# A transformer block on one core: pair sums of the last attention unit split between GpSimd and VectorE, and the projection's operands prepared in pieces

## The chip, the core and the metric

The kernel runs on one NeuronCore of a Trainium2 chip. TensorE (PE) does the matrix products, VectorE (DVE), ScalarE (ACT) and GpSimd (POOL) the elementwise work, and SyncE (SP) and ScalarE issue most of the DMA transfers. The metric is the device time of one launch in microseconds. Time before: 2572.67 us, the median of 3 runs (2571.6 to 2576.87). The profile is of one further execution of its own.

## The reference

The input x has B = 2 elements of T = 2048 rows and D = 512 columns, in float32; there are H = 16 heads of 32 columns.

```
mod = silu(condition) @ Wada + bada
sh_a, sc_a, gt_a, sh_m, sc_m, gt_m = split(mod, 6)
xm = layernorm(x) * (1 + sc_a) + sh_a
q, k, v = heads(xm @ Wqkv)
attn = softmax(where(causal, q @ k.T * 32**-0.5, -inf))
x = x + gt_a * ((attn @ v) @ Wproj + bproj)
xm = layernorm(x) * (1 + sc_m) + sh_m
x = x + gt_m * (gelu(xm @ W1 + b1) @ W2 + b2)
```

## The kernel before

**Stages.** For each batch element: queries, keys and values (class `Qkv`), attention (`attention_phase`, L481), and the output projection with the residual sum (`project_phase`, L849). The projection of element 0 runs together with the beginning of element 1's queries and keys, that of element 1 with the beginning of the feed-forward part, which comes last for both elements.

**Attention units.** The 16 heads form four groups c of four heads, and the 2048 query rows four blocks i of 512. A unit is one pair (c, i), in the order of `units` (L258); the last four are (3, 0), (3, 2), (3, 1), (3, 3), so `last_order` is 0, 2, 1, 3. The document counts blocks in this order: block 1 is i = 0, block 2 is i = 2, block 3 is i = 1, block 4 is i = 3. A unit goes through its key tiles of 128 rows in steps. The last unit has 15 steps, 0 to 14: twelve full ones, the diagonal one (12), a pair (13) and a half (14).

**A step** (`scores_t`, L488): for each head, PE first writes minus the row maximum into a PSUM bank of the tag st (from `fold`, which L466 makes once for each unit), then adds the transposed scores; ScalarE takes the exponential into a tile e (L526; 12 buffers, so three steps), and on the diagonal GpSimd masks it (L531). Two steps later PE multiplies e with the values into o. For the row sums, GpSimd adds the tiles of two neighbouring steps (`pair_sums`, L548, the addition is L551; 6 buffers ee), and PE sums the result over the rows into sm. `finish` (L561) copies o and sm out and stores them (od and sd in DRAM).

**Row maxima.** The scores in the other orientation are made ahead of their unit, piece by piece between the products of earlier steps (`score`, `bank`): PE writes a tile s, and VectorE takes its maximum (L407, on the diagonal L402). The last unit has none of this work left.

**What the projection needs.** The result of each block is divided by its row sums before it is multiplied with Wproj. `inverses` (L316) loads a block's sums as a tile r, inverts them (L328), stores them to DRAM (L329) and loads them back broadcast over the 32 columns of each head, in four transfers of 256 KB (L331), into a tile rb or into an old query tile (`old_queries`; the tag qst has 4 buffers). `prefetch` (L341), called at step 3 of the last unit, loads Wproj, the bias, x rows and the results of blocks 1 and 2, calls `inverses` for both on SyncE's queue, and multiplies each block as a whole (L373). `gate_weights` (L375), called at step 7, multiplies the bias and the four pieces of Wproj with the gate row (L378, L380; PE makes that row by a small product). In `project_phase` the inverses of blocks 3 and 4 are made on ScalarE's queue (L873) and multiplied in pieces of 512 columns (L892); for each 128 rows GpSimd adds the bias to x (L880), PE makes four products into ps_o, VectorE adds both (L887) and takes the statistics of the next normalization, and SyncE stores the result (L889).

**What sets the order.** A scheduler places the instructions of each engine by when it expects their operands; every instruction that passes through `mm`, `transpose` or `act` keeps the program's order on its engine. Each engine works through its queue in that order. DMA transfers of both queues take eight completion semaphores in turn: each waits for the one eight places before it.

Of the kernel before, what the change touches and what calls it, by code (L numbers as in the profile page):

```python
# [8 lines left out]
F32 = mybir.dt.float32  # L9
# [18 lines left out]
def dit_block_kernel(  # L28
# [32 lines left out]


    nc = tc.nc
    B, T, D = x.shape
# [10 lines left out]
    E_BUFS = 12  # L75
    EE_BUFS = 6
    AHEAD = 2
# [194 lines left out]
    class Row:  # L272
# [31 lines left out]
        def load_queries(self, u):  # L304
# [9 lines left out]
            self.qst[u] = t  # L314

        def inverses(self, i, rb, queue):  # L316

            sums, inv = [
                d[self.b][i].rearrange("c h (p q) -> (c h p) q", p=P // (C * HC))
                for d in (sd, rd)
            ]
            r = bp.tile([P, C * HC * QB // P], F32, tag="r", name="r", bufs=2)
            queue.dma_start(r, sums)
            nc.vector.reciprocal(r, r)  # L328
            queue.dma_start(inv, r)  # L329
            for c in range(C):  # L330
                queue.dma_start(  # L331
                    rb[:, c, :],
                    rd[self.b][i][c].unsqueeze(1).to_broadcast([HC, HD, QB]),
                )
# [6 lines left out]
        def prefetch(self):  # L341
# [27 lines left out]
            nc.sync.dma_start(self.at_s[1], od[b][last_order[1]])  # L369
            for k in range(2):  # L370
                rb = self.old_queries()
                self.inverses(last_order[k], rb, nc.sync)
                nc.vector.tensor_tensor(self.at_s[k], self.at_s[k], rb, ALU.mult)  # L373

        def gate_weights(self):  # L375

            ps = rows_of(ps_sp, 0, self.b, "s")
            nc.vector.tensor_tensor(bgate, bgate, ps, ALU.mult)  # L378
            for c in range(C):
                nc.vector.tensor_tensor(  # L380
                    self.wproj[:, c, :], self.wproj[:, c, :], ps, ALU.mult
                )

# [97 lines left out]
    def attention_phase(row):  # L481
        b, vv, kst, qst = row.b, row.vv, row.kst, row.qst
        with pool(f"att{b}") as ap, pool(
# [4 lines left out]
            def scores_t(u, step, n):  # L488
# [26 lines left out]
                for h in range(HC):  # L515
# [11 lines left out]
                    if tiles[0][0] >= i * TQ:  # L527

                        d = e.rearrange("p (t k) -> p t k", k=P)[:, 0 : TQ : TQ - 1, :]
                        d = d[:, : len(tiles), :]  # L530
                        nc.gpsimd.affine_select(  # L531
                            d, d, pattern=[[0, len(tiles)], [1, P]],
                            compare_op=ALU.is_ge, fill=0.0,
                            base=0, channel_multiplier=-1,
                        )
# [11 lines left out]

            def pair_sums(es0, es1):  # L548
                out = new_sums()
                for h in range(HC):  # L550
                    nc.gpsimd.tensor_tensor(out[h], es0[h], es1[h], ALU.add)  # L551
                return out
# [50 lines left out]
            for u, (c, i) in enumerate(units):  # L603
# [5 lines left out]
                for n_step, tiles in enumerate(steps_of[u]):  # L609
# [10 lines left out]
                    if u + 1 < len(units) and row.rows_made == u + 1:  # L620
                        if last:
                            row.score(row.count(cum[-1], u + 1))
                        make_rows = last or (ready > u + 1 and n_step >= 1)
                    if u == len(units) - 1 and n_step == 3:
                        row.prefetch()
                    if u == len(units) - 1 and n_step == 7:
                        row.gate_weights()
                    flush(now)
# [33 lines left out]
                    else:  # L662
                        ee = pair_sums(even, es)
                        pending.append(
# [184 lines left out]
    def project_phase(row, psum, between):  # L849
# [5 lines left out]
        with pool(f"proj{b}") as pp:  # L855
# [3 lines left out]
            for k, i in enumerate(last_order):  # L859
# [6 lines left out]
                for t in range(TQ):  # L866
                    if n in (0, TQ - 1):
                        d = 2 + n // (TQ - 1)
                        rbs[d] = (
                            row.old_queries() if d == 2  # L870
                            else pp.tile([P, C, QB], F32, tag="rb", name="rb")
                        )
                        row.inverses(last_order[d], rbs[d], nc.scalar)  # L873
                    nt = b * NT + i * TQ + t
# [502 lines left out]
```

## Time and profile before

| | us |
|---|---|
| median of 3 runs | 2572.67 |
| profiled execution: its own time | 2566.7 |
| profiled execution: span from the first to the last instruction | 2564.6 |
| PE busy in the span | 2502.6 (98%) |
| VectorE busy | 1301.8 (51%) |
| ScalarE busy | 895.4 (35%) |
| GpSimd busy | 845.1 (33%) |

The mean clock granted to PE is 0.989 of full speed. Times in the profile count from the start of the span; lines such as L551 are lines of the kernel before. The last two units of element 0 lie at about 690 to 826 us and its projection at 826 to 890; those of element 1 at 1550 to 1687 and 1687 to 1757. A busy PE is not PE at its peak, since matmuls are pipelined; what an edit is worth is read from the places where PE is idle or its clock is low, and from what ended the wait there.

### The profile page before, as it was taken

The page shows a single profiled execution, that of the slowest core. Times are in us where ns is not written, and L with a number is a line of the kernel's source. Part 1 is how long each engine was busy: PE and PEld are TensorE (multiplying, and loading weights), DVE is VectorE, ACT ScalarE, POOL GpSimd, SP SyncE. Part 2 cuts the span into 40 slices and gives each one's busy share as a digit, 9 for nine tenths or more (in the row PEclk, how much of TensorE's full clock was granted, in tenths as well). Part 3 has the DMA queues.
Part 4 walks back from the last instruction along what each step waited for, and adds up shares of the span by engine and source line. Part 5 has one row for each costly group of instructions (what it writes and reads, how often), then busy time and mean ns, then how long its engine had stood idle before and what let it go on. Part 6 is the DMA issues. An engine that isn't in the chain of part 4 may idle for free.

```text
span 2564.6 us, 31548 instructions
## 1 busy us (share of the span) xinstructions
PE 2502.6 (98%) x11361; PEld 1185.5 (46%) x11361; DVE 1301.8 (51%) x2732; ACT 895.4 (35%) x1667; POOL 845.1 (33%) x1038
## 2 busy tenths in 40 slices
PE   7999999999999999999999999899999999999998
PEld 3445445445443444454454445344444444444443
DVE  3455657666551635556665756245353344334424
ACT  1213455455545011254545454513312312311310
POOL 0001454544556366245545554632101100100100
PEclk9999999999999999999999999999999999999999
DMA  6645123041211798640414112144233332322422
GB/s 219 207 125 146 38 56 77 22 108 42 92 49 50 238 294 284 203 95 22 108 42 102 34 40 81 64 160 143 76 99 106 107 107 90 129 89 76 138 82 94
DMA packets 131718, 277.87 MB, mean 108 GB/s; under 512 B 13109, under 2 KB 41821, under 8 KB 127466
## 3 DMA queue, kind: packets, MB, share of 16 engines
q1 hardware_dynamic: 122818, 248.29, 32.7%
q0 software_dynamic: 5376, 23.07, 2.6%
q10 hardware_dynamic: 3368, 4.50, 0.5%
q8 instruction: 89, 1.46, 0.2%
q14 instruction: 67, 0.55, 0.1%
HBM read 201.90 MB, written 73.92 MB: 108 GB/s over the span
## 4 chain that ended last, share of the span: by engine, by line
PE 91%; DMA 4%; DVE 2%; issue 1%; POOL 1%; ACT 1%; SPq 0%; ACTq 0%; DVEq 0%; POOLq 0%
PE st L190 20%; PE ps_y L190 15%; PE ps_h L190 15%; PE o L190 10%; PE s L190 9%; PE ps_qk L190 8%; PE sm L190 6%; PE ps_v L190 4%; PE ps_o L190 2%; DMA rb<-r 1%; PE ps_xt L198 1%; DMA qst<-r 1%; DVE mx L407 1%; POOL ee L551 1%; PE ps_o L198 0%
## 5 line engine op out<-in xcount | busy, mean ns | idle before, releaser
L526 ACT ACTIVATE e<-st 128x512 f32<-128x512 f32 (+1 forms) x1152 | 575.5, 576 | 556.7 <-PE st L190 511.1
L551 POOL TENSOR_TENSOR ee<-e 128x512 f32<-128x512 f32 x384 | 489.3, 1305 | 423.1 <-ACT e L526 271.5
L407 DVE TENSOR_REDUCE mx<-s 128x1 f32<-128x512 f32 x616 | 413.8, 687 | 285.4 <-PE s L190 284.2
L190 PE MATMUL s<-kst,qst 128*128 128x512 f32 (+3 forms) x1058 | 451.3, 446 | 15.7 <-DVE mx L407 12.9
L190 PE MATMUL st<-qst,kst 128*128 128x512 f32 (+3 forms) x1280 | 435.4, 389 | 0.0
L190 PE MATMUL o<-e,vv 128*32 128x512 f32 (+3 forms) x2560 | 295.2, 542 | 0.0
L402 DVE CUSTOM_DVE_ANT_0 junk<-s,causal 128x384 bf16<-128x384 f32 (+3 forms) x442 | 211.3, 478 | 148.8 <-PE s L190 139.5
L190 PE MATMUL ps_h<-sx,w 128*128 128x512 f32 x640 | 286.7, 592 | 0.0
L190 PE MATMUL ps_y<-sh,w 128*128 128x512 f32 x640 | 277.8, 594 | 0.0
L190 PEld LDWEIGHTS st<-qst,kst 128*128 128x128 f32 x1280 | 227.8, 190 | 87.2 <-issue 62.8
L190 PEld LDWEIGHTS s<-kst,qst 128*128 128x128 f32 x1058 | 198.8, 189 | 140.5 <-DVE mx L407 57.5
L531 POOL TENSOR_SCALAR_AFFINE_SELECT e<-e 128x128 f32<-128x128 f32 (+1 forms) x384 | 124.9, 333 | 395.6 <-ACT e L526 389.2
L1148 POOL TENSOR_TENSOR c<-c 128x512 f32<-128x512 f32 x32 | 40.8, 1274 | 615.7 <-DVE c L1110 606.3
L190 PE MATMUL ps_qk<-xmT,wqkv 128*128 128x512 f32 x512 | 240.6, 598 | 2.2 <-DVE xmT L246 2.2
L1110 DVE TENSOR_TENSOR h<-c,ps_h 128x512 f32<-128x512 f32 x128 | 88.1, 688 | 231.4 <-PE ps_h L190 231.4
L190 PEld LDWEIGHTS ps_h<-sx,w 128*128 128x128 f32 x640 | 121.1, 190 | 150.2 <-issue 149.7
L190 PEld LDWEIGHTS ps_y<-sh,w 128*128 128x128 f32 x640 | 121.3, 191 | 148.5 <-issue 147.1
L190 PE MATMUL st<-fold,sel 32*128 32x512 f32 (+1 forms) x1152 | 162.4, 484 | 6.2 <-ACT e L526 3.8
L1134 ACT ACTIVATE h<-h,cols 128x512 f32<-128x512 f32 x128 | 92.4, 722 | 181.6 <-DVE h L1110 181.6
L190 PEld LDWEIGHTS st<-fold,sel 32*128 32x128 f32 x1152 | 64.6, 183 | 191.7 <-ACT e L526 110.0
L190 PEld LDWEIGHTS ps_qk<-xmT,wqkv 128*128 128x128 f32 x512 | 94.7, 191 | 97.6 <-issue 90.3
L190 PE MATMUL ps_v<-wqkv,xmT 128*128 128x512 f32 x256 | 122.8, 595 | 2.1 <-ACT xmT L251 2.1
(122 smaller groups left out, 2261.6 us busy)
## 6 DMA issues: line engine op xcount, KB each, us to landing
qst<-q SPq DMA_DIRECT2D x128, 256.0 KB
w<-w1d SPq DMA_DIRECT2D x34, 896.0 KB
w<-w2d SPq DMA_DIRECT2D x28, 1024.0 KB
kst<-k SPq DMA_DIRECT2D x24, 1024.0 KB
q<-hl SPq DMA_DIRECT2D x32, 512.0 KB
k<-hl SPq DMA_DIRECT2D x32, 512.0 KB
kst<-k SPq DMA_DIRECT2D x32, 256.0 KB
o<-ot SPq DMA_DIRECT2D x32, 256.0 KB
```

The costliest lines, as they stand in the source:

```text
L190: return tc.keep_in_program_order(nc.tensor.matmul(*args, **kw))
L198: return tc.keep_in_program_order(nc.tensor.transpose(dst, src, ident[:n, :n]))
L402: nc.vector.tensor_tensor_reduce(junk[:, :w], s[:, :w], causal[:, QB - w :], 1.0, MASKED, ALU.add, ALU.max, m,)
L407: nc.vector.tensor_reduce(m, s[:, :w], axis=AX.X, op=ALU.max)
L526: act(nc.scalar.activation(e[:, :w], sts[h][:, :w], AF.Exp))
L531: nc.gpsimd.affine_select(d, d, pattern=[[0, len(tiles)], [1, P]], compare_op=ALU.is_ge, fill=0.0, base=0, channel_multiplier=-1,)
L551: nc.gpsimd.tensor_tensor(out[h], es0[h], es1[h], ALU.add)
L1110: nc.vector.tensor_tensor(dst, x, y, op)
L1134: nc.scalar.activation(d, d, AF.Gelu, bias=col(r_b1 + chunk, 1))
L1148: nc.gpsimd.tensor_tensor(c1_, c1_, c2_, ALU.subtract)
```

## The change

In the last unit of each element VectorE does the pair sums of heads 1 and 3, and GpSimd those of heads 0 and 2. `prefetch` only loads, the sums of block 3 among them. A new function `prepare` spreads the rest over the steps of the last unit: at step 5 the reciprocals of blocks 1 to 3 with their stores, and the gate row; at steps 5 to 8 one piece of Wproj each; at step 7 the broadcasts for blocks 1 and 2; at steps 9 to 12 one piece of each of the two blocks. `inverses` is split into `load_sums`, `invert` and the broadcasts; for block 4 all three stay in the projection. The reciprocals, the multiplies, the masks and the pair sums keep the program's order on their engines. The tag ee has 12 buffers instead of 6, and r has 3 instead of 2.

```diff
@@ -73,7 +74,7 @@
     NG = T // MT
     LAG = 2
     E_BUFS = 12
-    EE_BUFS = 6
+    EE_BUFS = 12
     AHEAD = 2
     const = ctx.enter_context(tc.tile_pool(name="const", bufs=1))
@@ -313,20 +314,22 @@
                 )
             self.qst[u] = t
+        def load_sums(self, i, queue):
+            r = bp.tile([P, C * HC * QB // P], F32, tag="r", name="r", bufs=3)
+            queue.dma_start(
+                r, sd[self.b][i].rearrange("c h (p q) -> (c h p) q", p=P // (C * HC))
+            )
+            return r
+        def invert(self, i, r, queue):
+            act(nc.vector.reciprocal(r, r))
+            queue.dma_start(
+                rd[self.b][i].rearrange("c h (p q) -> (c h p) q", p=P // (C * HC)), r
+            )
         def inverses(self, i, rb, queue):
-            sums, inv = [
-                d[self.b][i].rearrange("c h (p q) -> (c h p) q", p=P // (C * HC))
-                for d in (sd, rd)
-            ]
-            r = bp.tile([P, C * HC * QB // P], F32, tag="r", name="r", bufs=2)
-            queue.dma_start(r, sums)
-            nc.vector.reciprocal(r, r)
-            queue.dma_start(inv, r)
             for c in range(C):
                 queue.dma_start(
                     rb[:, c, :],
@@ -367,19 +370,28 @@
                 else:
                     nc.sync.dma_start(self.next_s[t], x1d[t])
             nc.sync.dma_start(self.at_s[1], od[b][last_order[1]])
-            for k in range(2):
-                rb = self.old_queries()
-                self.inverses(last_order[k], rb, nc.sync)
-                nc.vector.tensor_tensor(self.at_s[k], self.at_s[k], rb, ALU.mult)
-        def gate_weights(self):
-            ps = rows_of(ps_sp, 0, self.b, "s")
-            nc.vector.tensor_tensor(bgate, bgate, ps, ALU.mult)
-            for c in range(C):
-                nc.vector.tensor_tensor(
-                    self.wproj[:, c, :], self.wproj[:, c, :], ps, ALU.mult
-                )
+            self.r_s = [self.load_sums(i, nc.sync) for i in last_order[:3]]
+        def prepare(self, n):
+            if n == 3:
+                self.prefetch()
+            elif n == 5:
+                for k in range(3):
+                    self.invert(last_order[k], self.r_s[k], nc.sync)
+                self.ps_gate = rows_of(ps_sp, 0, self.b, "s")
+                act(nc.vector.tensor_tensor(bgate, bgate, self.ps_gate, ALU.mult))
+            elif n == 7:
+                self.rb_s = [self.old_queries() for _ in range(2)]
+                for k in range(2):
+                    self.inverses(last_order[k], self.rb_s[k], nc.sync)
+            if 5 <= n < 5 + C:
+                w = self.wproj[:, n - 5, :]
+                act(nc.vector.tensor_tensor(w, w, self.ps_gate, ALU.mult))
+            elif 9 <= n < 9 + C:
+                for k in range(2):
+                    d, r = self.at_s[k][:, n - 9, :], self.rb_s[k][:, n - 9, :]
+                    act(nc.vector.tensor_tensor(d, d, r, ALU.mult))
         def width(self, u, h, t, kb):
             last = kb == units[u][1]
@@ -528,10 +540,12 @@
                         d = e.rearrange("p (t k) -> p t k", k=P)[:, 0 : TQ : TQ - 1, :]
                         d = d[:, : len(tiles), :]
-                        nc.gpsimd.affine_select(
-                            d, d, pattern=[[0, len(tiles)], [1, P]],
-                            compare_op=ALU.is_ge, fill=0.0,
-                            base=0, channel_multiplier=-1,
+                        act(
+                            nc.gpsimd.affine_select(
+                                d, d, pattern=[[0, len(tiles)], [1, P]],
+                                compare_op=ALU.is_ge, fill=0.0,
+                                base=0, channel_multiplier=-1,
+                            )
                         )
                     es.append(e)
                     if h >= HC - n:
@@ -545,10 +559,12 @@
                     for _ in range(HC)
                 ]
-            def pair_sums(es0, es1):
+            def pair_sums(u, es0, es1):
                 out = new_sums()
                 for h in range(HC):
-                    nc.gpsimd.tensor_tensor(out[h], es0[h], es1[h], ALU.add)
+                    vector = u == len(units) - 1 and h % 2
+                    engine = nc.vector if vector else nc.gpsimd
+                    act(engine.tensor_tensor(out[h], es0[h], es1[h], ALU.add))
                 return out
             def products(dst, lhs, es, q0, at, first, last):
@@ -621,10 +637,8 @@
                         if last:
                             row.score(row.count(cum[-1], u + 1))
                         make_rows = last or (ready > u + 1 and n_step >= 1)
-                    if u == len(units) - 1 and n_step == 3:
-                        row.prefetch()
-                    if u == len(units) - 1 and n_step == 7:
-                        row.gate_weights()
+                    if u == len(units) - 1:
+                        row.prepare(n_step)
                     flush(now)
                     if make_rows:
                         row.rows(u + 1)
@@ -660,7 +674,7 @@
                     elif n_step % 2 == 0:
                         even = es
                     else:
-                        ee = pair_sums(even, es)
+                        ee = pair_sums(u, even, es)
                         pending.append(
                             (
                                 now + LAG + 1,
@@ -870,6 +884,12 @@
                             row.old_queries() if d == 2
                             else pp.tile([P, C, QB], F32, tag="rb", name="rb")
                         )
+                        if d == 3:
+                            row.invert(
+                                last_order[d],
+                                row.load_sums(last_order[d], nc.scalar),
+                                nc.scalar,
+                            )
                         row.inverses(last_order[d], rbs[d], nc.scalar)
                     nt = b * NT + i * TQ + t
                     if k == 0:
```

## The prediction

> **What bounds the kernel now.** I read the page first (TensorE, PE, is busy 98% of a 2564.6 us span), then PE's busy time and granted clock in slices of 5 us over the whole span, then the chain of waits and the timelines of the slices where PE is not full. Outside the start and the end of the program, PE is idle for more than 0.6 us at a time in three places per batch element that the change touches, and after each the granted clock is below 1 for a while. Columns: slice, length, PE, PEld, DVE, ACT, POOL busy, clock, DMA share, GB/s.
>
> ```profile
> 740.00:745.00 5.00, 2.64 (x23) 1.48 (x15) 0.00 (x0) 2.06 (x4) 2.94 (x3) 1.00 0.25 97
> 745.00:750.00 5.00, 1.42 (x6) 0.67 (x10) 4.30 (x6) 0.00 (x0) 4.05 (x2) 0.56 0.00 2
> 750.00:755.00 5.00, 5.00 (x33) 2.47 (x37) 2.44 (x7) 3.09 (x6) 0.00 (x0) 0.76 0.16 56
> ...
> 800.00:805.00 5.00, 3.54 (x23) 1.38 (x19) 0.00 (x0) 1.93 (x4) 5.00 (x5) 1.00 0.02 9
> 805.00:810.00 5.00, 4.59 (x21) 1.46 (x21) 0.00 (x0) 2.42 (x5) 3.23 (x3) 0.70 0.02 3
> ...
> 855.00:860.00 5.00, 3.96 (x13) 1.76 (x11) 1.61 (x3) 0.00 (x0) 0.29 (x1) 1.00 0.49 178
> 860.00:865.00 5.00, 2.70 (x6) 1.56 (x7) 3.31 (x7) 0.00 (x0) 4.54 (x4) 0.67 0.64 202
> 865.00:870.00 5.00, 5.00 (x9) 2.03 (x8) 4.91 (x12) 0.00 (x0) 0.59 (x1) 0.65 0.86 302
> ```
>
> To be seen: stall A (742 to 749, in the last unit but one), stall B (803 to 806, inside the last unit), stall C (859 to 863, in the projection). Batch element 1 has the same three at 1601 to 1609, 1663 to 1666 and 1716 to 1722. The chain of waits says what ended A and B (start, us, what):
>
> ```profile
> 734.35 10.98 DMA qst<-r
> ...
> 745.62 0.13 DVE kst L373
> 745.75 2.10 issue
> 747.85 0.69 DVE mx L407
> 748.54 0.04 issue
> 748.58 1.39 PE s L190 x2
> ...
> 797.31 1.94 POOL kst L880 x2
> ...
> 802.28 2.46 POOL ee L551 x2
> 804.74 0.02 issue
> 804.76 0.61 ACT e L526
> ```
>
> A: VectorE's queue holds the multiply L373 in the middle of the score maxima (L407). It waits for the broadcast inverses, and PE waits for the maxima behind it. B: GpSimd was given the four bias adds (L880) between its pair sums (L551); the sums come late, their e buffers stay taken, and the exponentials and PE wait. C has two causes. In element 0, PE waits for L887, that for L880, that for an x load which SyncE issued at 854.12, when the third broadcast of block 4's inverses (rb) had landed. In element 1, VectorE stands in L892 until 1716.55 for the fourth rb, with L887 behind it.
>
> **The Trainium skill.** "TensorE: Matmul & The Clock Gate", What's actually happening: an idle window of some 3.4 us puts PE on half clock, and a busy one releases it. The trace agrees in kind: 0.56 and 0.76 behind stall A. "DMA: Bandwidth & Descriptors", Why a DMA increments its semaphore by 16 and not by 1: a transfer uses as many engines as divide its slowest dimension, the lowest-numbered ones. An inverse broadcast has 4 heads as slowest dimension, so all of them share 4 of 16 engines: the slice 740 to 745 shows a share of 0.25 and 97 GB/s. "SBUF — State Buffer", Who interferes with whom: a VectorE instruction with two SBUF inputs excludes a GpSimd one that reads SBUF. The trace agrees: four sums take 5.0 us alone and 6.98 us (from 742.07) beside the 2.31 us multiply.
>
> **The change, part by part.** What each stall costs: idle plus (1 - clock) x busy of the slow slices.
> - A: element 0: 2.36 + 3.58 = 5.94 idle, 0.44 x 1.42 + 0.24 x 5 = 1.82 of clock; element 1: 5.93 + 1.64. Sum 15.3 us.
> - B: 1.87 + 1.63 and 1.88 + 1.50. Sum 6.9 us.
> - C: element 0 3.34 + 2.64 = 6.0; element 1 4.88 + 2.12 = 7.0.
>
> Together 35.2 us: the ceiling.
>
> *Multiply and inverse out of the score work.* L373 (two of 2.3 us) becomes eight multiplies of 512 columns at steps 9 to 12 of the last unit, after the last maximum. In the compiled order of the changed kernel nothing on VectorE before the last unit's fold waits for a DMA of this preparation. A goes wholly: **-15.3**. Next late there would be VectorE itself, but it is busy 3.2 to 4.4 us of 5 in this stage, so it keeps up. Bounds: -13 (the clock part only half real) to -15.3.
>
> *Half of the sums to VectorE.* 24 sums a unit; GpSimd keeps 12. A pair of steps takes 6.3 to 6.6 us (exponentials from 777.75 to 784.03). GpSimd's load per pair falls from 4 x 1.25 = 5.0 to 2.5, plus 2 x about 0.65 for the exclusion, 3.8; the four bias adds (1.25 each) now stand two before and two after one sum. VectorE's sum is priced as L892 (512 columns, two SBUF inputs, 0.68): 1.4 per pair. The sum of step 5 must be read before step 7's exponential needs the buffer. Counted from the unit's first exponential (771.18), steps start about 0, 3.4, 6.6, 9.7, 12.9, 16.3, 19.4, 22.8, 26.0, 29.4, 32.5, 35.9, 39.0, 42.5, 45.4. The gate product of the bias (bgate) is ready at about 18.5, two adds end at 21.3, the sum behind them at 22.6; head 2 of step 7 needs it at 23.8. It fits by 1.2 us. I leave 0.4 for both elements: **-6.5**, bounds -3 and -6.9.
>
> *VectorE's queue in the last unit.* Behind the three reciprocals stand bgate, the weights and all later sums. The third needs block 3's sums: stored at 6.5, and loaded by about 10.2 (1.9 us from store to load and at most 1.85 to the reciprocal in this trace); VectorE reaches it at 12.4 to 13.9. No wait. SyncE then issues three stores and eight broadcasts; the first goes at about 14.4 (1.44 us after a store of inverses). Four broadcasts took 12.7 us from the first issue (732.61) to the last landing (745.33), of which 10.5 at 97 to 100 GB/s: 2.65 each. All eight use the same engines: landings at about 19, 22, 25, 27.5 and 30, 33, 35.5, 38. The multiplies ask for block 2's first piece before the sum of step 9 (29.4 to 31.5), and for its last at 38. Just in time: **0**, bounds 0 and +4.
>
> *Block 3's broadcasts.* They leave ScalarE's queue behind step 12's exponentials (about 41.1), since their buffer is the one that the multiplies have read; three issues of 0.53 stand before step 13's exponentials, and the last before step 14's. ScalarE is idle 1.1 to 1.5 us a step, and in the trace these issues ran beside exponentials: **0**, bounds 0 and +2. They land by 4 us into the projection; their use is at 8.
>
> *Block 4's inverses in program order.* The reciprocal moves from behind one or two to behind three blocks of 128 rows: from 5.2 (831.69 - 826.48) to about 14 in element 0, from 6.7 to about 12 in element 1. With it move the store and four broadcasts. Element 0: stage by stage the inverse store lands near 17, rb 0 to 2 at about 24, 27, 30. But the x loads now wait for rb 0, 1 (or for none) instead of rb 2, 3 (each DMA waits for the one eight before it, and the order moved): x at 28 instead of 33. L887 can go at about 31; PE needed it at 32.5. Stall nearly gone: **-5.0**, bounds -6 and +2. Element 1: the broadcasts start at 14, not 8.7. Before, they took 20.7 us, at 4.1 each under other loads: (256 KB + a sixteenth of 3.4 MB) per engine at 25 GB/s is 19 us. With some 2.5 MB beside them now, 16.6 + 2.1: the last lands at about 33, not 29.4. Four multiplies (L892) that wait for it stand before the second L887 of the second block, and PE's transpose needs the normalization some 3.4 us behind: PE goes on at 36.4 instead of 34.3. Stall C of element 1 grows: **+2.8** with its clock, bounds -7 and +6.
>
> *Buffers, and the fixed order of GpSimd.* Twelve sum buffers remove GpSimd's waits for PE (1.5 to 1.8 us before a group of sums), which ended nothing on PE. Masks now come after four pending sums instead of two: 2.5 us later, with two steps of 3.4 to 3.8 us in hand. **0**, bounds 0 and +2.
>
> Sum: -15.3 - 6.5 - 5.0 + 2.8 = **-24.0 us**. Against the profiled execution: 2566.7 - 24.0 = 2542.7. The median of the runs shown, 2572.67, is 6.0 above that execution; so **2549 us**.
>
> **The rivals.**
> R1, both C stalls vanish: the rb broadcasts of element 1 run at 2.65, land at 27, and the x loads no longer wait for them. For it: 8 x 2.65 is what the trace shows when nothing else loads. Against: loads of 2 MB fall into the same time. -15.3 - 6.9 - 6 - 7 = -35: 2538.
> R2, B stays in another form: a VectorE sum behind a waiting reciprocal or multiply holds the e buffers as L880 did, or GpSimd loses more to the exclusion. For it: margins of 1.2 us. -15.3 + 0 - 3 + 3 = about -15: 2557.
> R3, slower: block 3's first broadcast sits in ScalarE's in-order queue, waiting for VectorE's last multiply of block 1 and for block 2's broadcasts; the last two steps' exponentials are behind it, and PE behind them. It costs as soon as the eighth broadcast lands after 41. At 4.9 us a broadcast instead of 2.65 it lands at 14.4 + 2.1 + 39 = 56, PE stands 15 us in each element: -24 + 30 = +6, 2579. For it: 4.1 each was seen in the projection. Against: in the last unit the DMA share is 0.02 to 0.26, so nothing slows them.
> R4, no change: a wait of the same size as A appears in the projection, about 2572.
>
> **How the numbers follow.** Forecast 0.58, R1 0.14, R2 0.18, R3 0.06, R4 0.04. The forecast, R1 and R2 are faster by over 0.2% (5 us, about what a measurement of this kernel can tell from no change): 0.90; same 0.04; slower 0.06. The range takes in R1 and R2: 2537 to 2561.
>
> **What would show it.** A right: no slice under 4.9 of PE in the last unit but one, and VectorE's only waits there are for PE. B right: no exponential waits for a sum in the last unit. Broadcast step right: eight landings 2.65 us apart, share 0.26 for 21 us. C: in element 0 PE full around 33 us into the projection, in element 1 a stall of 5 to 9 us ended by L892 waiting for rb. Wrong if ScalarE waits at its broadcasts, or if sums on VectorE stand behind a DMA.

## The result, and the profile after

The changed kernel takes 2557.38 us, the median of 5 runs (2556.07 to 2561.76), beside 2571.74 us for the kernel before (5 runs, 2570.12 to 2576.87): 0.9943 of its time, with a 95% interval of 0.9929 to 0.9958. That is 14.4 us faster; 24.0 were forecast. The profiled execution took 2558.56 us, with a span of 2556.7 us. The profiled execution of the kernel before was faster than all its timed runs (2566.7 against 2570.12 and more), so the two profiles differ by 7.9 us only, and the sum of the steps has to be compared with 7.9, not with 14.4. In which stage the timed runs of the kernel before lose the other 5 us, no trace shows.

PE's time can be cut at its own events into stages that add up to the span: the 15 attention units ahead of the last one of each element (from the first turned maximum of the first unit to that of the last), the last unit (to the first ps_o), the projection (first to last ps_o). What lies between hardly changes: the start 223.8 and 224.8, queries and keys of element 1 195.5 and 197.0, everything after its projection 811.7 in both. How far one profile can be trusted is seen from the two kernels that were profiled twice (the changed kernel and e9, e7 and e10): they differ by at most 0.9 us in the 15 units, 0.2 in the last unit, 2.4 in the projection and 3.8 in the queries and keys of element 1, which take 195.3 to 203.2 us in the fourteen profiles. The table has all kernels of this study, element 0 / element 1, in us:

| kernel | 15 units | last unit | projection | ratio to before, 95% |
|---|---|---|---|---|
| before | 539.3 / 538.4 | 63.4 / 63.6 | 63.1 / 65.8 | 1 |
| changed | 535.8 / 534.8 | 59.6 / 59.6 | 62.6 / 70.8 | 0.9943 (0.9929 to 0.9958) |
| e1 free reciprocal | 535.2 / 535.0 | 59.6 / 59.6 | 63.1 / 65.3 | 0.9943 (0.9922 to 0.9963) |
| e2 broadcasts by head | 534.5 / 534.4 | 62.2 / 62.2 | 57.9 / 58.7 | 0.9905 (0.9890 to 0.9920) |
| e3 before, 12 buffers | 543.6 / 542.2 | 60.1 / 60.0 | 63.4 / 66.3 | 0.9985 (0.9976 to 0.9994) |
| e4 buffers split | 531.5 / 531.8 | 65.3 / 65.2 | 62.5 / 71.9 | 0.9968 (0.9955 to 0.9980) |
| e5 sums on GpSimd | 534.5 / 535.4 | 71.0 / 71.3 | 63.4 / 70.3 | 1.0044 (1.0030 to 1.0058) |
| e6 before, by head | 533.1 / 534.1 | 66.4 / 66.7 | 57.0 / 58.6 | 0.9942 (0.9928 to 0.9955) |
| e7 buffers by head | 531.7 / 531.8 | 59.7 / 59.6 | 63.9 / 70.4 | 0.9936 (0.9921 to 0.9951) |
| e8 e7 and e2 together | 531.6 / 529.0 | 60.1 / 60.2 | 57.5 / 58.6 | 0.9861 (0.9845 to 0.9878) |
| e9 changed again | 535.0 / 534.9 | 59.8 / 59.6 | 62.5 / 73.2 | 0.9945 (0.9932 to 0.9959) |
| e10 e7 again | 532.3 / 532.7 | 59.6 / 59.6 | 62.4 / 70.2 | 0.9936 (0.9924 to 0.9949) |
| e11 e8 without the moves | 532.9 / 534.8 | 65.9 / 65.7 | 57.5 / 58.7 | 0.9922 (0.9910 to 0.9935) |
| e12 e11, gate at step 5 | 533.7 / 534.3 | 59.4 / 59.5 | 56.8 / 58.6 | 0.9878 (0.9858 to 0.9897) |

The slices of the changed kernel that answer to those of before (slice, length, busy time of PE, PEld, DVE, ACT and POOL, clock, DMA share, GB/s):

```profile
740.00:745.00 5.00, 5.00 (x45) 2.47 (x41) 3.10 (x6) 2.08 (x4) 0.00 (x0) 1.00 0.00 0
745.00:750.00 5.00, 4.98 (x50) 2.52 (x41) 2.69 (x6) 2.76 (x6) 2.75 (x3) 1.00 0.01 3
...
800.00:805.00 5.00, 5.00 (x34) 2.23 (x31) 5.00 (x6) 2.65 (x6) 2.17 (x2) 1.00 0.27 105
...
850.00:855.00 5.00, 2.64 (x10) 1.16 (x8) 1.41 (x2) 0.00 (x0) 1.03 (x1) 1.00 0.56 184
855.00:860.00 5.00, 2.98 (x7) 1.59 (x8) 4.45 (x9) 0.00 (x0) 4.35 (x4) 0.72 0.57 186
```

A and B are gone: PE is full in 740 to 750 and in 800 to 805, at full clock. The unit that held A, the last of the 15, took 59.3 and 59.0 us and takes 51.6 in both elements (from its first turned maximum to that of the next). C is still there, 4.4 us of idle PE in element 0. In element 1 it is 10 us, where it was 4.9:

```profile
1700.00:1705.00 5.00, 3.45 (x9) 1.29 (x7) 0.79 (x2) 0.00 (x0) 0.00 (x0) 1.00 0.82 261
1705.00:1710.00 5.00, 0.00 (x0) 0.00 (x0) 0.59 (x1) 0.00 (x0) 0.00 (x0) 0.71 0.22 85
1710.00:1715.00 5.00, 1.51 (x7) 1.51 (x8) 4.84 (x10) 1.13 (x2) 0.35 (x1) 0.50 0.36 114
```

Its chain of waits (start, us, what; `r<-r` is the store of the inverted sums, `rb<-r` a broadcast of them) reads:

```profile
1687.27 3.61 DMA r<-r
...
1692.75 17.36 DMA rb<-r
...
1710.74 0.68 DVE xt L907
```

The store of the inverses takes 3.6 us, then the last broadcast lands 17.4 us after it was issued, and the normalization of the next rows (L907 of the changed kernel, L887 before) stands on VectorE behind the multiplies that wait for it.

The table shows one thing more, which no step of the forecast had. The unit that held A lost 7.7 and 7.4 us, but the 15 units together lost only 3.5 and 3.6. Two units in each element became longer: both took 52.8 us and take 54.3 (the first of element 0 from 403.15 to 457.48; the expectations below count the second together with the unit of 21.1 us ahead of it, as 74.0 and 75.5). In the first of them PE is idle for 1.07 us, where it was for 0.02. The chain of the changed kernel there:

```profile
451.61 0.22 DVE m L431
451.83 0.20 DVE junk L414
452.03 0.01 DVE mx L414
452.04 0.94 DVE mhl L433
452.98 0.02 issue
453.00 1.21 DVE mhl L434
454.20 0.33 DVE junk L414
```

L433 and L434 split the maxima of the next unit into a rounded part and the rest, 128 x 16 elements each (L421 and L422 before). Their median is 0.17 and 0.18 us, and here they take 0.94 and 1.21. Score maxima stand behind them, and PE behind these. GpSimd's timeline tells what differs. First the changed kernel, then the kernel before:

```profile
449.16 5.01 POOL L567 TENSOR_TENSOR ee<-e 128x512 f32<-128x512 f32 x4 [2.76 <-ACT e L538]
454.11 1.05 POOL L544 TENSOR_SCALAR_AFFINE_SELECT e<-e 128x128 f32<-128x128 f32 x4
```

```profile
447.03 2.53 POOL L551 TENSOR_TENSOR ee<-e 128x512 f32<-128x512 f32 x2 [2.74 <-ACT e L526]
451.14 0.29 POOL L531 TENSOR_SCALAR_AFFINE_SELECT e<-e 128x128 f32<-128x128 f32 x1 [1.58 <-ACT e L526]
...
453.11 2.52 POOL L551 TENSOR_TENSOR ee<-e 128x512 f32<-128x512 f32 x2 [0.19 <-PE sm L190]
```

With 6 buffers the last two sums of the pair of steps wait for PE (sm), and masks go first. The split fell into that gap, at 449.8. With 12 buffers four sums of 1.25 us go in one go, and the split falls among them: L433 is over at 452.98 and L434 at 454.2, when the third and the fourth of the sums end.

The collision itself isn't new. In the kernel before the split is as slow in three other units of each element, in element 0 at 356.5, 507.8 and 659.2 us:

```profile
356.52 1.29 DVE L421 CAST mhl<-m 128x16 fp32r<-128x16 f32 x1
357.85 1.22 DVE L422 TENSOR_TENSOR mhl<-m,mhl 128x16 fp32r<-128x16 f32 x1
```

There no maximum follows it directly on VectorE. The units around it take 59.4 to 59.7 us, and as long in the changed kernel, where the split has no sum beside it. So the collision costs time by its place: the change moved it in front of maxima that PE waits for.

### The profile page after: what moved, and what is told of

The parts are those of the page before. It is cut to its first block, busy times and chain, and to the rows that moved or that the text cites. A ratio compares the mean times of both kernels' runs of the same rounds, so it can differ in the third digit from the quotient of the medians.

```text
span 2556.7 us, 31466 instructions
## 1 busy us (share of the span) xinstructions
PE 2497.3 (98%) x11361; PEld 1186.6 (46%) x11361; DVE 1335.4 (52%) x2768; ACT 894.6 (35%) x1667; POOL 813.9 (32%) x1014
## 4 chain that ended last, share of the span: by engine, by line
PE 92%; DVE 3%; DMA 3%; ACT 1%; issue 1%; ACTq 0%; POOL 0%; SPq 0%; DVEq 0%
PE st L191 20%; PE ps_y L191 15%; PE ps_h L191 15%; PE o L191 10%; PE s L191 9%; PE ps_qk L191 8%; PE sm L191 6%; PE ps_v L191 4%; PE ps_o L191 3%; PE ps_xt L199 1%; DMA rb<-r 1%; DVE mx L419 1%; DVE junk L414 1%; DMA k<-hl 1%; PE ps_o L199 0%
## 5 line engine op out<-in xcount | busy, mean ns | idle before, releaser
L538 ACT ACTIVATE e<-st 128x512 f32<-128x512 f32 (+1 forms) x1152 | 575.1, 576 | 556.8 <-PE st L191 519.5
L567 POOL TENSOR_TENSOR ee<-e 128x512 f32<-128x512 f32 x360 | 457.8, 1304 | 417.4 <-ACT e L538 413.9
```

The costliest lines, as they stand in the source:

```text
L538: act(nc.scalar.activation(e[:, :w], sts[h][:, :w], AF.Exp))
L567: act(engine.tensor_tensor(out[h], es0[h], es1[h], ALU.add))
```

## The experiments

Kernels of one group below ran on the same chip, beside the kernel before: e1 to e4, e5 to e8, e9 to e11, and e12 alone.

**e1, the reciprocal of block 4 not held in program order.**

```diff
-        def invert(self, i, r, queue):
-            act(nc.vector.reciprocal(r, r))
+        def invert(self, i, r, queue, keep=act):
+            keep(nc.vector.reciprocal(r, r))
...
                                 nc.scalar,
+                                keep=lambda ins: ins,
```

> The changed kernel with one thing taken back: the reciprocal of block 4's sums isn't held in program order any more, so the scheduler puts it some 17 VectorE instructions earlier, as before the change. Theory (the held reciprocal delays the inverses, and in element 1 the fourth broadcast rb ends the stall): in element 1 the reciprocal runs near 1681 instead of 1686.7, the fourth broadcast lands some 5 us before 1710, and PE's idle time in the projection falls from 10.0 to about 5 us; in element 0 the x load is what ends the stall, which shrinks by 0 to 3 us. Time 5 us under the changed kernel's 2557.4: about 2552. Rival (the broadcasts are slow because x loads share their DMA engines, whenever they start): the landing stays near 1710 and the time within 1 us of 2557.4.

Measured: 2554.59 us; its ratio equals that of the changed kernel, and the interval is too wide to tell 5 us. The stages do tell: the projection of element 1 takes 65.3 us, not 70.8 (73.2 in e9), idle PE there falls from 10.0 to 4.7 us, and the fourth broadcast, issued at 1682.6, lands at 1701.3, 29.3 us into the projection instead of 35.9. That of element 0 stays (63.1 and 62.6): the first broadcast goes 5 us sooner, 14.0 us into the projection instead of 19.2, but the x load that PE waits for is issued behind the second one, 29.8 us in instead of 26.8. So holding the reciprocal costs 5.5 us in element 1 and nothing in element 0. The broadcast itself still takes 18.6 us.

**e2, broadcasts cut by head.**

```diff
-            for c in range(C):
+            for h in range(HC):
                 queue.dma_start(
-                    rb[:, c, :],
-                    rd[self.b][i][c].unsqueeze(1).to_broadcast([HC, HD, QB]),
+                    rb[h * HD : (h + 1) * HD, :, :],
+                    rd[self.b][i][:, h, :].unsqueeze(0).to_broadcast([HD, C, QB]),
```

> The changed kernel with the four broadcasts of each block's inverses cut by head (32 partitions, four chunks each) instead of by chunk (128 partitions from four rows). The same bytes, the same values. Theory (a broadcast by chunk keeps only 4 of the 16 DMA engines busy, so that its landing, not its issue, makes stall C): the four broadcasts of block 4 land within 5 to 7 us of their issue instead of 12.7 and more; in element 1 the fourth lands near 1698 instead of 1710, in element 0 the x loads behind it start 8 us sooner; idle time of PE in the two projections falls from 4.4 and 10.0 to 1 or less each, and the clock loss with it: 13 to 15 us, about 2543.5. Rival (the x loads beside them use up the bandwidth, so that the cut doesn't matter): landings as before, time within 2 us of 2557.4.

Measured: 2548.92 us. C is gone as a stall: the projections take 57.9 and 58.7 us, 4.7 and 12.1 less than in the changed kernel, and in element 1 no slice of 5 us has more than 0.2 us of idle PE:

```profile
1700.00:1705.00 5.00, 5.00 (x19) 2.61 (x18) 3.17 (x8) 1.05 (x2) 1.03 (x1) 1.00 0.98 318
1705.00:1710.00 5.00, 5.00 (x13) 2.28 (x12) 3.84 (x8) 0.08 (x1) 2.28 (x1) 1.00 0.91 339
```

In the last unit 2.6 us per element came back: PE was idle for 0.31 us in 804 to 805, and from 806 to 809 its clock was 0.50 to 0.55; it was 0.50 to 0.58 for as long in element 1 too. This is the difference between 2543.5 and the time measured. The cause of C is the landing of broadcasts, and with it of the x loads behind them: in element 0 the x load is issued 18.5 us into the projection instead of 26.8. In element 1 the scheduler moved the four multiplies later as well, but the fourth broadcast, issued at 1698.1, is used at 1706.3 without a wait, 8.2 us later. At the 17.4 us of the changed kernel it would have held them.

**e3, the kernel before with 12 buffers.**

```diff
-    EE_BUFS = 6
+    EE_BUFS = 12
```

> The kernel before with one number changed: 12 buffers for the pair sums instead of 6. Everything else of the change is left out. Theory (with free buffers the scheduler puts pair sums ahead of masks on GpSimd, and one of these sums then lies beside VectorE's split of the maxima, which goes from 0.17 to about 1.1 us each, twice, ahead of the score products of the next unit): the two units 401 to 454 and 531 to 605 us and their twins in element 1 grow by 1.5 us each, +6 in all. In the last unit the bias adds move behind 15 sums, which may take away some of stall B, 0 to -6.5. Stalls A and C stay as in the kernel before. Time 2571.7 + 6 - 3 = about 2575, between 2571 and 2578. Rival (the longer units come from another part of the change, the buffers are neutral in these units): units of 52.8 and 74.0 us as before, and a time of 2571.7 or, if B shrinks, down to 2565.

Measured: 2569.81 us, a little faster than before. The stages show both halves of what was expected: the 15 units are 4.3 and 3.8 us longer (403.1 to 457.4 is 54.3 us again), the last unit 3.3 and 3.6 us shorter. The longer units come from the buffers alone; nothing else of the change is in this kernel. Also: stall B goes without VectorE's help once the scheduler may put 15 sums ahead of the first bias add.

**e4, the twelve buffers split, six and six.** Masks and sums keep program order in the last unit only.

```diff
-    EE_BUFS = 12
+    EE_BUFS = 6
...
+            def keep(u):
+                return act if u == len(units) - 1 else (lambda ins: ins)
...
-                    ap.tile([P, QB], F32, tag="ee", name="ee", bufs=EE_BUFS)
+                    ap.tile([P, QB], F32, tag=f"ee{u == len(units) - 1}", name="ee", bufs=EE_BUFS)
```

> The changed kernel with its twelve buffers for sums split, six for the last unit and six for all others, and masks and sums held in program order in the last unit alone: in all other units GpSimd then gets the order of the kernel before (masks before the last two sums), in the last unit that of the changed kernel up to four bias adds between the same sums. Theory (the order of sums and masks made the four long units): units of 52.8 and 74.0 us again instead of 54.3 and 75.5, A and B stay away, time 2557.4 - 6.2 = about 2551. Rival (the long units come from a shift in time through other parts of the change): units stay at 54.3 and 75.5, time within 1 us of 2557.4.

Measured: 2563.57 us, slower than the changed kernel. The 15 units are at 531.5 and 531.8, 4.3 and 3.0 us shorter, and the four long units are at 52.8 us again. With e3 this shows that the buffers, by the order of sums and masks that they allow, made them long. But the last unit is 5.7 and 5.6 us longer. Its chain at stall B's place (L906 are the bias adds, L573 the sums):

```profile
781.48 2.78 POOL kst L906 x2
...
784.42 3.02 POOL kst L906 x2
787.43 1.68 POOL ee L573
...
789.14 0.61 ACT e L538
```

Four bias adds, 5.8 us of GpSimd, stand ahead of a sum for whose buffer the exponential waits. With six buffers B stays although VectorE has half of the sums. Later ScalarE stood 3.4 us in front of its broadcasts for block 3, which wait for VectorE's last multiply of block 1: the place of rival R3.

**e5, all sums of the last unit on GpSimd.**

```diff
-                    vector = u == len(units) - 1 and h % 2
+                    vector = False
```

> The changed kernel with the sums of the last unit all on GpSimd again; twelve buffers, the fixed order and all else stay. GpSimd's order in that unit is then 12 sums, four bias adds, 12 sums. Theory (twelve buffers alone end stall B, since a late sum no longer keeps an exponential from its buffer): the last unit stays at 59.6 us or within 1 us of it, time 2557 within 2. Rival (it took VectorE's half of the sums): GpSimd with 24 x 1.25 + 4 x 1.25 = 35 us of sums and adds and the masks has no slack over the unit, the sums before the last products come late and PE waits 3 us or more in each element, 2563 or more.

Measured: 2580.22 us, slower than the kernel before; the last unit takes 71.0 us. The time is the rival's, the mechanism isn't. ScalarE's timeline in the last unit (start, us, what; in brackets the idle time before and what ended it; L334 are the broadcasts, L538 the exponentials):

```profile
800.64 1.20 ACTq L334 DMA_DIRECT2D qst<-r  x2
801.94 0.60 ACT L538 ACTIVATE e<-st 128x512 f32<-128x512 f32 x1 [11.20 <-DVE kst L394]
```

This is R3 in full: ScalarE was idle for 11.2 us at the broadcasts for block 3, with the exponentials behind them. They waited for VectorE's multiplies (L394), which started at 789.7, beside bias adds and sums on GpSimd without a gap, and took 1.75 us each (median) instead of the 0.68 of the changed kernel. But slow multiplies are only one half of it. The edit also let the scheduler move the broadcasts: in ScalarE's queue they stand ahead of step 8's exponentials here, of step 13's in the changed kernel, in both elements. What each half costs was not tried, and this kernel can't say whether GpSimd alone would have kept up.

**e6, the kernel before with broadcasts by head.** The edit of e2, in the kernel before.

> The kernel before with the broadcasts of the inverses cut by head, nothing else of the change. The scheduler then also puts VectorE's first multiply L373 eight score maxima later in its queue. Theory (stalls A and C are the landing of broadcasts that use 4 of the 16 DMA engines): four broadcasts land within 5 us of the first issue instead of 12.7, A falls from 7.7 us an element with its clock to 1 or less, C from 6.0 and 7.0 to 1 or less, B stays at 3.5 an element: 2572.2 - 13 - 11 = about 2548. Rival (A is the place of the two 2.3 us multiplies among the maxima, also if they wait for nothing): half of A stays, about 2555.

Measured: 2554.67 us: this one edit gives what the whole change gives (0.9942 and 0.9943). DMA in 1 us slices of this kernel, from the first issue at 733.4:

```profile
735.00:736.00 1.00, 1.00 (x16) 0.15 (x7) 0.00 (x0) 0.00 (x0) 0.00 (x0) 1.00 0.88 225
736.00:737.00 1.00, 1.00 (x9) 0.48 (x6) 0.00 (x0) 0.00 (x0) 0.00 (x0) 1.00 1.05 260
```

The share is 0.85 to 1.05 up to 739, and the four broadcasts are over at about 740, 6.5 us after their first issue; before, they ran at 0.26 and 102 GB/s to 745.3, 12.7 us after theirs. The 15 units lose 6.2 and 4.3 us, the projections 6.1 and 7.2. A has 0.7 us of idle left, and its unit takes 52.8 us instead of 59.3 and 59.0; C has 0.4 in element 0 and nothing in element 1. Of the expected 24 us 13.6 came (the kernel before takes 2568.27 us in this group). The largest part of what is missing is B, which grew by 3 us per element (66.4 and 66.7 for the last unit); why it grew was not tried.

For A the edit did two things, since the scheduler also put the multiply eight score maxima later in VectorE's queue. There it waits for nothing:

```profile
749.09 2.28 DVE L373 TENSOR_TENSOR kst<-kst,qst 128x2048 f32<-128x2048 f32 x1
```

Broadcasts as slow as before, 12.7 us from 733.4, would have landed at 746 and not held it at this place either; at its old place, some 8 us earlier, it would have met broadcasts that had just landed (both are estimates from these times). So e6 shows that a multiply of 2.3 us among the maxima costs little when it waits for nothing (52.8 us for the unit, against 51.6 in the changed kernel). Whether the faster landing or the later place ended the wait, it does not tell apart.

**e7, twelve buffers in the last unit, six elsewhere**, by heads, on top of e4:

```diff
-                        tag=f"ee{u == len(units) - 1}",
+                        tag=f"ee{u == len(units) - 1 and h >= HC // 2}",
```

> As the split of six and six, but in the last unit heads 0 and 1 take their sums from the six buffers of all other units and heads 2 and 3 from six of their own, so that the last unit has twelve and all others have six. Order on GpSimd as in the split, the four bias adds in a row between 6 and 6 sums. Theory (the split lost 6 us because the last unit had six buffers, and the bias adds held it up): units of 52.8 and 74.0 us, no slice of PE under 4.7 in the last unit, time 2557.4 - 6.2 = about 2551. Rival (four bias adds in a row are what cost): the slice 785 to 790 stays at 3.3, and the time above 2556.

Measured: 2553.23 us. The last unit is back at 59.7 and 59.6, the 15 units stay at 531.7 and 531.8. The bias adds stand in a row as in e4, so it was the buffers that were short there: 11.2 us between the last units of e4 and e7. VectorE's timeline at the place shown above, in this kernel:

```profile
450.22 0.17 DVE L433 CAST mhl<-m 128x16 fp32r<-128x16 f32 x1
450.43 0.18 DVE L434 TENSOR_TENSOR mhl<-m,mhl 128x16 fp32r<-128x16 f32 x1
```

GpSimd does nothing from 449.95 to 451.54 there. The same instructions take 0.35 us, not 2.2.

**e8, e7 and e2 together.**

> The changed kernel with both repairs: broadcasts by head, and the buffers by head of the last unit's sums. Theory (the two losses are independent): C at 1 us or less in both elements, units of 52.8 and 74.0 us, 2548.9 - 6.2 = about 2543. Rival (the earlier broadcasts meet the bias adds and the sums in a new way, B returns): 2546 to 2549, with a slice of PE under 4.0 in the last unit.

Measured: 2533.52 us, the fastest kernel of this study, 0.9861 of before. The units are repaired, the projections take 57.5 and 58.6, and the last unit 60.1: the half clock that e2 had after its 0.31 us of idle PE is not seen here, after 0.30. The end of element 1's queries and keys happens to leave the clock at 1.00 too, where e7 had 0.56 and 0.76 in two slices (3.4 us). Against the 9.5 us below what was expected stand three things: 3.9 us are the group's, since the kernel before takes 2568.27 us beside e8 and took 2572.16 beside e2; the last units are 2.1 and 2.0 us shorter than in e2; and the 3.4 us of clock, which e2 had lost too. Together that is more than enough, but the last two are read from one profile.

**e9 and e10, the changed kernel and e7 once more, side by side.**

> The changed kernel itself once more, so that it stands beside the two kernels that follow on one chip. 0.9943 of the kernel before again, within 0.0015; units of 54.3 and 75.5 us, stall C of 4 and 10 us. No theory says otherwise.

> The changed kernel with the buffers by head once more. Theory (the order of sums and masks costs 6.2 us in the changed kernel): 6 us, or 0.0024 of the time, under the changed kernel's run beside it, so 0.9919 of the kernel before. Rival (these 6 us are given back elsewhere, as the last run's 0.9936 would allow): within 2 us of the changed kernel.

Measured: 2556.69 and 2554.01 us, 2.7 apart. e9 repeats the changed kernel (0.9945, long units of 54.3 to 54.4 us). By time this is inconclusive: the intervals overlap, and neither 6 nor 2 us can be excluded. By units it is clear: each of the four long units takes 52.8 to 52.9 us in e7 and e10, as before the change, and 54.3 to 54.4 in both profiles of the changed kernel, 6.1 us in all. What hides this in the time lies elsewhere: the first unit of an element takes 6.0 to 7.4 us in one kernel or another, 7.3 and 6.0 in the two profiles of the changed kernel's element 0, and the queries and keys of element 1 took 195.3 and 199.1 us in the two profiles of e7's kernel.

**e11, without the moves.** The kernel before with the edits of e2, VectorE's sums and the buffers of e7; `prefetch` and `gate_weights` are those of before.

> The kernel before with three things: broadcasts by head, VectorE's half of the sums in the last unit (masks and sums held in order there), and the buffers by head. Inverses, gate, weights and multiplies stay as in the kernel before: the part of the change that moves the preparation into the last unit is left out. Theory (with fast landings the moves are worth little: A has 0.7 us and its clock left, C 0.4): 2533.5 + 3 or 4 = about 2537, 0.988 of the kernel before. Rival (the two 2.3 us multiplies, now beside the sums on VectorE in the last unit, hold sums and exponentials): 2543 or more, with slices of PE under 4.0 in the last unit.

Measured: 2550.35 us: the rival's time, again with another mechanism. A is 0.7 us, C 0.7, but B is back, 2.9 us of idle and a half clock after it. The two long multiplies are not in its chain (L378 is the gate product, L890 the bias adds, L561 the sums):

```profile
789.65 0.70 DVE bgate L378
790.35 0.07 issue
790.42 2.52 POOL kst L890 x2
792.94 1.68 POOL ee L561
794.62 3.37 POOL kst L890 x2
```

The bias adds start 33.4 us into the unit (757.0), because the gate product is made at step 7. GpSimd waits 5.4 us for it, with sums behind. (In e3 the product is made at step 7 too, and B is gone: there the sums aren't held in program order, and 15 of them go ahead.) In the changed kernel, where `prepare` makes the product at step 5, they start 26.8 us into the unit (787.4).

**e12, the gate and the weights at step 5.**

```diff
-                    if u == len(units) - 1 and n_step == 7:
+                    if u == len(units) - 1 and n_step == 5:
```

> The last kernel with one number changed: gate and weights at step 5 of the last unit instead of step 7. Theory (what is left of B there is the bias adds that GpSimd starts at 790.4, 33 us into the unit, because they wait for the gate; the place of the inverses and multiplies is worth little): bias adds start near 783, the slice 795 to 800 goes from 2.10 to above 4.6, about 6 us gone in each element: 2550.35 - 12 = about 2538, 0.9875 of the kernel before. Rival (bias adds in a row between sums cost wherever they stand, or the two 2.3 us multiplies hold VectorE's sums): the stall moves to 785 to 795, and the time stays within 3 us of 2550.

Measured: 2537.61 us. The slices at the places of A and B:

```profile
750.00:755.00 5.00, 4.28 (x22) 1.82 (x23) 5.00 (x9) 2.08 (x4) 3.15 (x2) 1.00 0.46 187
...
795.00:800.00 5.00, 5.00 (x32) 2.17 (x32) 3.05 (x2) 3.10 (x7) 2.98 (x2) 1.00 0.10 25
```

B is gone. A's 0.7 us and 0.2 us at C in element 0 are what is left of the three stalls. The inverses and the multiplies of the blocks stand where they stood before the change; only the gate and the weights have moved. Beside e8, which moves all of them, no difference is shown: 0.9878 (0.9858 to 0.9897) against 0.9861 (0.9845 to 0.9878).

## Why the prediction was half right

Right: the sign, and A and B with their sizes. The range holds the time, but at its slow end, and for a reason that it did not give.

*A (forecast -15.3).* Right: the unit that held it lost 7.7 and 7.4 us, -15.2, and has 0.02 us of idle PE left. That the multiplies waited for the landing of the broadcasts is in the chain that the prediction shows; e6 shows that without the wait 0.7 us stays.

*B (-6.5).* Right in size: 63.4 and 63.6 became 59.6 and 59.6, -7.8, a little beyond the bound of -6.9, and the rest is not traced. But "Half of the sums to VectorE" isn't the whole cause. With VectorE's half and 6 buffers B stays (e4), with VectorE's half, its fixed order and a gate at step 7 it stays (e11), and with 12 buffers and all sums on GpSimd it goes in the kernel before (e3). What the step did not name, the buffers, and what it took as given, the gate at step 5, each can decide it.

*C, element 0 (-5.0; measured -0.5).* The terms that were mis-sized are the store and the x load. Expected were the inverse store at 17 us into the projection, the first broadcast at 24, x at 28; the trace has (`xt<-in_x_dram` is the x load):

```profile
835.32 4.03 DMA r<-r
...
839.38 7.54 DMA rb<-r
...
846.93 6.96 DMA xt<-in_x_dram
```

That is 19.2, 26.8 and 33.7: the store ends 2.2 us late, and the load takes 7 us, not 4, beside the broadcasts still under way. So the stall of 4.4 us stayed.

*C, element 1 (+2.8; measured +5.0).* The mechanism is right, and e1 shows it by undoing it. The store was taken too short: it took 3.6 us, not 1.4, so the first broadcast went out 17.3 us into the projection instead of 14, and the fourth landed at 35.9 instead of 33. The broadcasts themselves took 18.6 us from the first issue to the last landing, as forecast (18.7).

*"Buffers, and the fixed order of GpSimd: 0, bounds 0 and +2".* This is the step that failed: it put at nothing what cost 6.1 us. It looked at what GpSimd waits for, found that these waits end nothing on PE, and priced their removal at nothing. But at two places in each element the wait had kept sums and VectorE's split apart, with maxima and PE behind the split. Removed, it costs 1.5 us at each of the four places (e3 has it alone; e4 and e7 take it back). In the last unit the same buffers are worth 11.2 us (e4 against e7), which the forecast did not price apart from B. The step even named masks behind four sums instead of two; it didn't ask what VectorE does meanwhile.

The sum: -15.2 from A, -7.8 from B, +6.1 from the four units, -0.5 and +5.0 from the projections, and +4.5 from the start, from the queries and keys of element 1 and from other units, which differ between executions of one kernel too: -7.9 of the span. The forecast had -24.0. Of the 16 us between, 6.1 are the buffers, 6.7 the two sizes of C and 4.5 the difference between executions; B gave 1.3 back. Against the medians of the runs the change is -14.4, since the profiled execution of before lay 5 us below its median and that of after 1 us above. That the range holds the time is in part luck: what was wrong in the buffers and in C stands in no rival, and only the width that R2 gives the range takes it in.

*The signs.* As forecast, no exponential waits for a sum in the last unit, and the DMA share is 0.22 to 0.27 from 785 to 805 us. One sign of being wrong did appear: VectorE's first multiply of block 2 waits 2.4 us for its broadcast in element 0 and 2.8 in element 1, with two sums behind it. It cost nothing: PE is full there.

*R2* (2557) has the right time, for a reason that isn't its own: B did not stay. *R3* did not happen in the changed kernel, where ScalarE's broadcasts go at 809.9 without holding an exponential, but it is real: in e5 it takes 11.2 us, with the broadcasts five steps earlier in ScalarE's queue and the multiplies at 1.75 us. *R1* is what e2 does by another way. *R4* is out.

**The Trainium skill** on these points. "DMA: Bandwidth & Descriptors", Why a DMA increments its semaphore by 16 and not by 1: how many DMA engines a transfer uses follows from the slowest dimension of its patterns. e6 agrees: slowest dimension 4, share 0.26; 32, share 0.85 to 1.05, and half the time. "SBUF — State Buffer", Who interferes with whom: the port pair that VectorE and GpSimd share is an exclusive lock. The trace agrees, and gives the price for a small instruction: 0.17 us became 0.94, 0.18 became 1.21, about one sum of 1.25 us each.

## What to carry to other kernels

Before preparation is moved out of the way of a late transfer, ask why the transfer is late: a DMA share of 0.26 at a stall said it here, and three edited lines gave as much as the whole change. A wait that ends nothing on the critical engine may still keep two other engines apart, and a collision that costs nothing at one place costs time at another; when buffers are added, read the order that each engine gets in every unit, not only in the one that the edit is meant for. And where a stall has several causes in a row (buffers, a late operand, an engine's load), taking one away may end it (e3) or show nothing (e4, e11), so try them in pairs too.

## What was not expected of the hardware

A VectorE instruction on 128 x 16 elements can take as long as GpSimd's sum of 128 x 512 beside it: 1.21 us against 0.18. Eight multiplies of 512 columns beside GpSimd without gaps took 1.75 us each (median) instead of 0.68. And 0.31 us of idle PE in the records was followed by some 3 us of half clock in e2, in both elements, but not by any in e8 after 0.30. That is far less than the idle window of 3.4 us that the prediction names, and A's 0.7 us in e6 was followed by none; what decides it was not tried.
